# A graph-attention layer with residual and norm: x of the last four blocks loaded earlier, top-8 and largest norm moved in the drain, the stores of blocks 0 to 25 issued twice

## The chip, the core and the metric

One core of a Trainium2 chip. The metric is the time of one execution in microseconds (us), the median of several runs. A profiled run also gives the span, from the first to the last instruction; here a run's time is mostly 1.9 us above its span. The drain is what comes after the last turn of the loop over the blocks. All runs used here are in the fast state.

## The reference

```python
def reference(x, adj, L0_gnn_W, L0_gnn_a):      # x 4096 x 512, adj 4096 x 4096, all float32
    ht  = (x @ W).reshape(N, 4, 512)            # four heads
    e   = leaky_relu(src_i + dst_j) + adj       # adj up to 1e9: the largest entry of a row decides
    att = softmax(e, axis=-1)
    out = layernorm(x + (att @ ht).mean(heads))
```

Entries of adj reach 1e9. On this data the largest one of a row is so far ahead that softmax is 1 there and 0 elsewhere. The kernel therefore finds the column of each row's largest entry, gathers that row of x, multiplies it by the mean of the heads' weights, adds x and normalizes. A test at the end, which needs the two largest entries of each row and a bound from the norms of x, decides whether a slow general path must run. It does not run on this data.

## The kernel before

The 4096 rows are 32 blocks of 128. Per block: VectorE takes the maximum of each of 64 segments (`segment_maxima`), finds the leading segment, GpSimd gathers it, VectorE finds the column in it, GpSimd gathers that row of x as `y`, TensorE transposes `y` and multiplies it, ScalarE computes the statistics and writes the result over x in `hold`. Nearly all loads and stores are issued by SyncE, in program order. The code is cut and condensed:

```python
AHEAD, Q, PIECES, LATE = 5, 4, 4, NB - Q

def load_x(lo, n):
    nc.sync.dma_start(hold[:, ds(lo, n), :], x_rows[:, ds(lo, n), :])

def find_inner(ib):
    nc.vector.max(out=inner[:, ib, :], in_=lead_of[ib])          # top-8 of the leading segment

def find_column(ib):
    find_inner(ib)
    within = small.tile([P, 8], U32, name="within")
    nc.vector.max_index(within, inner[:, ib, :], lead_of.pop(ib))
    ...                                                          # column, then gather_rows

def store(queue, lo, n):
    queue.dma_start(out_rows[:, ds(lo, n), :], hold[:, ds(lo, n), :])
...
for t in range(NB):
    if t in x_at:
        load_x(*x_at[t])
    load_adj(t + AHEAD)
    ...

load_x(LATE, NB - LATE)                     # the drain begins here
for ib in range(NB - FINISH):               # blocks 0 to 25
    store(nc.sync, ib, 1)
find_column(NB - 2)
...
for ib in range(LATE, NB):
    row_norm(ib)                            # sums of squares of x, ScalarE
turn(NB - 2)
products(NB - 3, KB - 1, KB)
finish_last(NB - 4, True)                   # True: VectorE adds x first
find_inner(NB - 1)
bound(0)                                    # largest norm: VectorE reduces, TensorE transposes
products(NB - 2)
...
finish_last(NB - 2, True)
store(nc.sync, NB - 2, 1)
report(pg)
finish_last(NB - 1, False)
store(nc.scalar, NB - 1, 1)                 # the last store is issued by ScalarE
```

Of the kernel before, what the change touches and what calls it, by code (L numbers as in the profile page):

```python
# [65 lines left out]
def leading_rows(ctx, tc, x, adj, W, a, out, ident, v, n_bad, any_bad):  # L66
# [7 lines left out]
    nc = tc.nc  # L74
    N, D = x.shape
    H = a.shape[0]
    KB, NB, S = D // P, N // P, N // E
    AHEAD = 5
    Q = 4
    PIECES = 4  # L80
    LATE = NB - Q
# [20 lines left out]
    def pieces(ib):  # L102
        return PIECES if ib in (0, LATE, NB - 1) else 2 if ib > LATE else 1

    def load_adj(ib):
        if 0 <= ib < NB:
            t = adj_t[ib] = adj_pool.tile([P, N], F32, name="adj_t")
            n = pieces(ib)
            for k in range(n):
                nc.sync.dma_start(t[:, ts(k, N // n)], adj_rows[ib][:, ts(k, N // n)])  # L110

    def load_x(lo, n):
        nc.sync.dma_start(hold[:, ds(lo, n), :], x_rows[:, ds(lo, n), :])
# [26 lines left out]
    top = once.tile([P, NB, 8], F32, name="top")  # L140
    inner = once.tile([P, NB, 8], F32, name="inner")
# [5 lines left out]
    seg_of, at_of, lead_of, y_t, yt_of, o_ps = {}, {}, {}, {}, {}, {}  # L147

    def segment_maxima(ib, lo, hi):

        if lo == 0:
            seg_of[ib] = small.tile([P, S], F32, name="seg")
        n = max(pieces(ib), 2)
        for k in range(lo * n // PIECES, hi * n // PIECES):
            nc.vector.tensor_reduce(  # L155
                seg_of[ib][:, ts(k, S // n)],
                adj_t[ib][:, ts(k, N // n)].rearrange("p (s e) -> p s e", e=E), axis=AX.X, op=OP.max,
            )

    def find_segment(ib):  # L160
        seg = seg_of.pop(ib)
        nc.vector.max(out=top[:, ib, :], in_=seg)
        at = small.tile([P, 8], U32, name="at")
        nc.vector.max_index(at, top[:, ib, :], seg)  # L164
        row = small.tile([P, 1], U32, name="row")
        nc.gpsimd.tensor_tensor(row, at[:, 0:1], first[:, ib : ib + 1], op=OP.add)  # L166
        lead = small.tile([P, E], F32, name="lead")
        nc.gpsimd.indirect_dma_start(  # L168
            out=lead, out_offset=None, in_=adj_segs,
            in_offset=bass.IndirectOffsetOnAxis(ap=row[:, :1], axis=0),  # L170
        )
        start = at_of[ib] = small.tile([P, 1], U32, name="start")
        nc.gpsimd.tensor_tensor(start, at[:, 0:1], width, op=OP.mult)  # L173
        lead_of[ib] = lead

    def gather_rows(ib, col):
        y = y_t[ib] = rows.tile([P, D], F32, name="y", bufs=4)
        nc.gpsimd.indirect_dma_start(  # L178
            out=y, out_offset=None, in_=x,
            in_offset=bass.IndirectOffsetOnAxis(ap=col[:, :1], axis=0),  # L180
        )

    def find_inner(ib):
        nc.vector.max(out=inner[:, ib, :], in_=lead_of[ib])

    def find_column(ib):
        find_inner(ib)
        within = small.tile([P, 8], U32, name="within")
        nc.vector.max_index(within, inner[:, ib, :], lead_of.pop(ib))  # L189
        col = small.tile([P, 1], U32, name="col")  # L190
        nc.gpsimd.tensor_tensor(col, at_of.pop(ib), within[:, 0:1], op=OP.add)  # L191
        gather_rows(ib, col)

    def find_column_in_row(ib):

        col = small.tile([P, 8], U32, name="col")
        nc.vector.max_index(col, top[:, ib, :], adj_t[ib])
        gather_rows(ib, col)
# [9 lines left out]
    def residual(ib):  # L208
        o_ps[ib] = psum.tile([P, D], F32, name="o")
        nc.tensor.matmul(o_ps[ib], ident, hold[:, ib, :], start=True, stop=False)  # L210

    def products(ib, lo=0, hi=KB):
        start = ib not in o_ps
        if start:
            o_ps[ib] = psum.tile([P, D], F32, name="o")
        for kb in range(lo, hi):
            nc.tensor.matmul(  # L217
                o_ps[ib], yt_of[ib][:, kb, :], w_sum[:, kb, :],
                start=(start and kb == 0), stop=(kb == KB - 1),
            )  # L220

    def row_norm(ib):
        sq = rows.tile([P, D], F32, name="sq")
        nc.scalar.activation(sq, hold[:, ib, :], AF.Square, accum_out=xx[:, ib : ib + 1])  # L224
# [8 lines left out]
    def rstd(i):  # L233
        nc.gpsimd.tensor_scalar(sd[:, i], sd[:, i], 1.0 / D, EPS, op0=OP.mult, op1=OP.add)  # L234
        nc.gpsimd.tensor_tensor(sd[:, i], sd[:, i], power[:, : i.stop - i.start], op=OP.pow)  # L235
        nc.gpsimd.tensor_mul(nm[:, i], nm[:, i], sd[:, i])  # L236
# [5 lines left out]
    def finish_last(ib, residual):  # L242

        o = o_ps.pop(ib)
        if residual:
            nc.vector.tensor_add(hold[:, ib, :], o, hold[:, ib, :])
            o = hold[:, ib, :]
        st = small.tile([P, nc.vector.BN_STATS_DIM], F32, name="st", bufs=2)
        nc.vector.bn_stats(st, o)
        mv = small.tile([P, nc.vector.BN_AGGR_DIM], F32, name="mv", bufs=2)  # L250
        nc.vector.bn_aggr(mv, st)
        r = small.tile([P, 1], F32, name="r", bufs=2)
        nc.scalar.activation(r, mv[:, 1:2], AF.Sqrt, bias=eps)
        nc.vector.reciprocal(r, r)
        nc.vector.tensor_scalar(hold[:, ib, :], o, mv[:, 0:1], r, op0=OP.subtract, op1=OP.mult)  # L255

    def store(queue, lo, n):
        queue.dma_start(out_rows[:, ds(lo, n), :], hold[:, ds(lo, n), :])

    def mean_of_heads(kb):  # L260
        o = psum.tile([P, D], F32, name="o")
        for h in range(H):
            nc.tensor.matmul(o, ident, hold[:, w_at + kb * H + h, :], start=(h == 0), stop=(h == H - 1))  # L263
        nc.scalar.activation(w_sum[:, kb, :], o, AF.Copy, scale=1.0 / H)  # L264
# [43 lines left out]
    def bound(part):  # L308

        if part == 0:  # L310
            xm = once.tile([P, 1], F32, name="xm")
            nc.vector.tensor_reduce(xm, xx, axis=AX.X, op=OP.max)
            px = of_bound[0] = psum.tile([1, P], F32, name="px", bufs=1)
            nc.tensor.transpose(px, xm, ident)
        elif part == 1:
            nc.vector.tensor_reduce(xg, of_bound[0], axis=AX.X, op=OP.max)
            nc.scalar.activation(xg, xg, AF.Sqrt)
            pb = of_bound[1] = psum.tile([P, 1], F32, name="px", bufs=1)
            nc.tensor.matmul(pb, ones[0:1, :], xg, start=True, stop=True)
        else:  # L320
            nc.vector.tensor_mul(lead_by, of_bound[1], vn)
            nc.vector.tensor_scalar(lead_by, lead_by, 1.05, 110.0, op0=OP.mult, op1=OP.add)
# [28 lines left out]
    COLUMN, PROJECT, STATS, FINISH = 2, 3, 4, 6  # L351

    for t in range(NB):
        if t in x_at:
            load_x(*x_at[t])
        load_adj(t + AHEAD)
        middle = 1 if t == NB - 1 else 2
        segment_maxima(t, 0, middle)
        if t >= COLUMN:
            find_column(t - COLUMN)  # L360
        segment_maxima(t, middle, PIECES)
        find_segment(t)
        pair = t >= FINISH and t % 2 == 0
        if pair:
            rstd(slice(t - FINISH, t - FINISH + 2))
        if t < 2:
            mean_of_heads(t)
        elif t == 2:
            mean_of_heads(2)
            mean_of_heads(3)  # L370
        if t == 0:
            turn_a()
        turned = [(*vectors[0], turn_w(*vectors.pop(0))) for _ in range(vectors_at.get(t, 0))]
        if t == 16:
            head_norms()
        ib = t - PROJECT
        if ib >= 0:
            turn(ib)
            if ib < LATE:
                residual(ib)  # L380
        for some in turned:
            head_vector(*some)
        if ib >= 0:
            products(ib)
        if t >= STATS:
            stats(t - STATS)
            row_norm(t - STATS)
        if pair:
            finish(t - FINISH)
            finish(t - FINISH + 1)  # L390

    load_x(LATE, NB - LATE)
    for ib in range(NB - FINISH):
        store(nc.sync, ib, 1)
    find_column(NB - 2)
    rstd(slice(NB - FINISH, NB - FINISH + 2))
    find_column_in_row(NB - 1)
    turn(NB - 3)
    products(NB - 3, 0, KB - 1)
    finish(NB - FINISH)  # L400
    finish(NB - FINISH + 1)
    for ib in range(LATE, NB):
        row_norm(ib)
    turn(NB - 2)
    products(NB - 3, KB - 1, KB)
    finish_last(NB - 4, True)
    find_inner(NB - 1)
    bound(0)
    products(NB - 2)
    bound(1)  # L410
    finish_last(NB - 3, True)
    bound(2)
# [249 lines left out]
```

## Time and profile before

| | before |
|---|---|
| time, median | 247.81 us (first 3 runs), 247.84 (6 runs) |
| span of the profiled run | 245.3 us |
| moved by DMA | 97.77 MB, of it 8.39 written |
| DMA engines | full from the second to the 38th of 40 slices |
| TensorE / VectorE / ScalarE / GpSimd busy | 82 / 77 / 45 / 40% |

How to read it: the page cuts the span into 40 slices and gives the busy share in tenths, with the rate of the DMA engines below. "Windows" are the same for chosen stretches. "(x24)" counts 24 instructions, and the five engines of a windows line are TensorE, TensorE's weight loads, VectorE, ScalarE and GpSimd. SyncE only issues transfers, so its own time says little; what moves is seen in the rates. In a waits line stand the microseconds in total, the number of waits and the longest.

### The profile page before, as it was taken

Reading aid. Unit: us, or ns where it says so; the run is one execution under the profiler, and the core shown is the slowest. Engines: PE = TensorE matmul, PEld = TensorE weight load, DVE = VectorE, ACT = ScalarE, POOL = GpSimd, SP = SyncE. Lnnn points to the kernel's source line nnn. Section 1 sums busy time; section 2 is a strip of 40 time slices with the busy share of each in tenths; the row PEclk is TensorE's granted clock in tenths of the full one; section 3 lists DMA queues with packets and bytes.
Section 4 is the critical chain, followed back from the end, with each engine's and each line's share of the span. In section 5 each row is a group of like instructions: output and inputs, shape, how many; then the busy total and the mean of one; then the engine's idle time right before and its main releaser. Section 6 shows DMA issues by size and latency. Waiting matters only on the chain.

```text
span 245.3 us, 2538 instructions
## 1 busy us (share of the span) xinstructions
PE 200.4 (82%) x677; PEld 101.2 (41%) x678; DVE 188.7 (77%) x300; ACT 110.1 (45%) x266; POOL 97.6 (40%) x213
## 2 busy tenths in 40 slices
PE   0279948999999999999969777985969987987870
PEld 0135326555665555665334323332424432433320
DVE  2545686399689977998589979995998999966661
ACT  2012004044656565657645463744553846657110
POOL 1202423225616463646254535453455455652000
PEclk9999799599999999999999999999988999999995
DMA  7999999999999999999999999999999999999971
GB/s 257 435 428 414 422 423 425 418 424 408 425 416 415 415 414 422 422 402 431 418 418 413 426 412 421 408 424 416 416 414 390 412 408 400 409 401 376 402 294 55
DMA packets 16580, 97.77 MB, mean 399 GB/s; under 512 B 2472, under 2 KB 2472, under 8 KB 11184
## 3 DMA queue, kind: packets, MB, share of 16 engines
q1 hardware_dynamic: 12816, 87.82, 87.4%
q0 software_dynamic: 3584, 9.44, 10.0%
q10 hardware_dynamic: 160, 0.28, 0.3%
q8 instruction: 7, 0.11, 0.2%
q14 instruction: 13, 0.11, 0.1%
HBM read 89.15 MB, written 8.39 MB: 398 GB/s over the span
## 4 chain that ended last, share of the span: by engine, by line
DMA 35%; issue 26%; POOL 25%; DVE 7%; PE 4%; SPq 1%; POOLq 0%; ACT 0%; DVEq 0%
DMA adj_t<-in_adj_dram 29%; POOL y L178 8%; POOL lead L168 8%; DVE seg L155 5%; DMA lead<-in_adj_dram,row 3%; PE o L217 3%; DMA y<-in_x_dram,col 3%; POOL sd L235 3%; POOL row L166 2%; POOL start L173 2%; POOL col L191 1%; POOL sd L234 1%; POOL nm L236 1%; DVE hold L255 1%; SPq L110 1%
## 5 line engine op out<-in xcount | busy, mean ns | idle before, releaser
L155 DVE TENSOR_REDUCE seg<-adj_t 128x32 f32<-128x2048 f32 (+1 forms) x70 | 146.0, 2091 | 34.7 <-DMA adj_t<-in_adj_dram 34.5
L217 PE MATMUL o<-w_sum,yt 128*128 128x512 f32 x256 | 120.6, 613 | 1.3 <-ACT yt L206 1.3
L217 PEld LDWEIGHTS o<-w_sum,yt 128*128 128x128 f32 x256 | 47.1, 194 | 59.7 <-issue 47.0
L206 ACT COPY yt<-tp 128x512 f32<-128x512 f32 x32 | 18.8, 588 | 45.0 <-PE tp L204 44.9
L178 POOL DMA_INDIRECT y<-in_x_dram,col x32 | 32.2, 1008 | 16.7 <-POOL col L191 14.6
L168 POOL DMA_INDIRECT lead<-in_adj_dram,row x32 | 30.9, 964 | 15.5 <-POOL row L166 15.5
L204 PE MATMUL tp<-ident,y 128*128 128x128 f32 x128 | 19.7, 276 | 15.5 <-DMA y<-in_x_dram,col 15.3
L210 PE MATMUL o<-hold,ident 128*128 128x512 f32 x58 | 31.6, 627 | 0.8 <-DMA hold<-in_x_dram 0.8
L263 PE MATMUL o<-hold,ident 128*128 128x512 f32 x32 | 18.3, 724 | 15.7 <-DMA hold<-in_L_gnn_W_dram 15.7
L204 PEld LDWEIGHTS tp<-ident,y 128*128 128x128 f32 x128 | 14.4, 141 | 28.8 <-issue 27.4
L166 POOL TENSOR_TENSOR row<-at,first 128x1 uint32<-128x1 uint32 x32 | 5.9, 185 | 48.6 <-DVE at L164 47.4
L281 ACT COPY wt<-tp 128x512 f32<-128x512 f32 x16 | 9.2, 587 | 35.8 <-PE tp L279 35.8
L191 POOL TENSOR_TENSOR col<-start,within 128x1 uint32<-128x1 uint32 x31 | 5.9, 190 | 41.6 <-DVE within L189 41.6
L240 ACT ACTIVATE hold<-o,nm,sd 128x512 f32<-128x512 f32 x28 | 20.2, 771 | 2.5 <-POOL nm L236 2.5
L287 PEld LDWEIGHTS pv<-at_d,wt 128*128 128x128 f32 x128 | 17.2, 200 | 7.4 <-issue 3.9
L224 ACT ACTIVATE sq<-hold 128x512 f32<-128x512 f32 x32 | 19.8, 620 | 0.0
L231 ACT ACTIVATE sq<-o,nm 128x512 f32<-128x512 f32 x28 | 19.3, 688 | 0.9
L263 PEld LDWEIGHTS o<-hold,ident 128*128 128x128 f32 x32 | 7.2, 236 | 24.2 <-POOL row L166 10.4
L229 ACT ACTIVATE sq<-o 128x512 f32<-128x512 f32 x28 | 17.0, 607 | 0.0
L264 ACT ACTIVATE w_sum<-o 128x512 f32<-128x512 f32 x4 | 2.4, 598 | 31.7 <-PE o L263 31.7
L287 PE MATMUL pv<-at_d,wt 128*128 128x2 f32 x128 | 16.0, 249 | 0.6 <-ACT wt L281 0.6
L279 PEld LDWEIGHTS tp<-ident,hold 128*128 128x128 f32 x64 | 7.9, 142 | 6.9 <-issue 6.9
(73 smaller groups left out, 116.7 us busy)
## 6 DMA issues: line engine op xcount, KB each, us to landing
adj_t<-in_adj_dram SPq DMA_DIRECT2D x27, 2048.0 KB
out_dram<-hold SPq DMA_DIRECT2D x31, 256.0 KB
hold<-in_x_dram SPq DMA_DIRECT2D x7, 1024.0 KB
adj_t<-in_adj_dram SPq DMA_DIRECT2D x12, 512.0 KB
hold<-in_L_gnn_W_dram SPq DMA_DIRECT2D x4, 1024.0 KB
adj_t<-in_adj_dram SPq DMA_DIRECT2D x4, 1024.0 KB
hold<-in_x_dram SPq DMA_DIRECT2D x4, 256.0 KB
lead<-in_adj_dram,row POOLq DMA_INDIRECT x32, 5.8
```

The costliest lines, as they stand in the source:

```text
L155: nc.vector.tensor_reduce(seg_of[ib][:, ts(k, S // n)], adj_t[ib][:, ts(k, N // n)].rearrange("p (s e) -> p s e", e=E), axis=AX.X, op=OP.max,)
L168: nc.gpsimd.indirect_dma_start(out=lead, out_offset=None, in_=adj_segs, in_offset=bass.IndirectOffsetOnAxis(ap=row[:, :1], axis=0),)
L178: nc.gpsimd.indirect_dma_start(out=y, out_offset=None, in_=x, in_offset=bass.IndirectOffsetOnAxis(ap=col[:, :1], axis=0),)
L204: nc.tensor.transpose(tp[:, kb, :], y[:, ts(kb, P)], ident)
L206: nc.scalar.copy(yt, tp)
L210: nc.tensor.matmul(o_ps[ib], ident, hold[:, ib, :], start=True, stop=False)
L217: nc.tensor.matmul(o_ps[ib], yt_of[ib][:, kb, :], w_sum[:, kb, :], start=(start and kb == 0), stop=(kb == KB - 1),)
L224: nc.scalar.activation(sq, hold[:, ib, :], AF.Square, accum_out=xx[:, ib : ib + 1])
L231: nc.scalar.activation(sq, o, AF.Square, bias=nm[:, i], accum_out=sd[:, i])
L240: nc.scalar.activation(hold[:, ib, :], o_ps.pop(ib), AF.Identity, bias=nm[:, i], scale=sd[:, i])
L263: nc.tensor.matmul(o, ident, hold[:, w_at + kb * H + h, :], start=(h == 0), stop=(h == H - 1))
L287: nc.tensor.matmul(pv[:, kb, h : 2 * H : H], wt[:, k, :], at_d[:, k, h : 2 * H : H], start=(k == 0), stop=(k == KB - 1),)
```

## The change

The stated intent: x of the last four blocks comes in front of the last block of adj, so that TensorE can add it for block 28 within the loop; the top-8 of the late blocks' leading segments leaves the path of the searches; the reduction behind the largest norm runs before block 28's statistics, so that TensorE does not wait for it.

```diff
     def find_column(ib):
-        find_inner(ib)
+        if ib < LATE:
+            find_inner(ib)
         within = small.tile([P, 8], U32, name="within")
-        nc.vector.max_index(within, inner[:, ib, :], lead_of.pop(ib))
+        nc.vector.max_index(within, top[:, ib, :], lead_of[ib])
 ...
+        if t + AHEAD == NB - 1:
+            load_x(LATE, NB - LATE)
         load_adj(t + AHEAD)
 ...
-            if ib < LATE:
-                residual(ib)
+            residual(ib)
 ...
-    load_x(LATE, NB - LATE)
     for ib in range(NB - FINISH):
         store(nc.sync, ib, 1)
     find_column(NB - 2)
     rstd(slice(NB - FINISH, NB - FINISH + 2))
+    for ib in range(LATE, NB):
+        row_norm(ib)
+    for ib in range(NB - FINISH):
+        store(nc.sync, ib, 1)
     find_column_in_row(NB - 1)
 ...
-    for ib in range(LATE, NB):
-        row_norm(ib)
     turn(NB - 2)
     products(NB - 3, KB - 1, KB)
-    finish_last(NB - 4, True)
-    find_inner(NB - 1)
     bound(0)
     products(NB - 2)
+    finish_last(NB - 4, False)
+    for ib in range(LATE, NB):
+        find_inner(ib)
     bound(1)
```

## The prediction

> **What bounds the kernel now.** I read the page's strip of slices first, then its list of DMA issues, then the windows of the last stretch, and the chain of waits last. That order matters here: the chain alone points at the wrong resource for this change. The strip and the DMA parts of the page:
>
> ```profile
> DMA  7999999999999999999999999999999999999971
> GB/s 257 435 428 414 422 423 425 418 424 408 425 416 415 415 414 422 422 402 431 418 418 413 426 412 421 408 424 416 416 414 390 412 408 400 409 401 376 402 294 55
> DMA packets 16580, 97.77 MB, mean 399 GB/s; under 512 B 2472, under 2 KB 2472, under 8 KB 11184
> ...
> HBM read 89.15 MB, written 8.39 MB: 398 GB/s over the span
> ...
> out_dram<-hold SPq DMA_DIRECT2D x31, 256.0 KB
> ```
>
> The 16 DMA engines are full in every slice but the first and the last two (a slice is 245.3 / 40 = 6.13 us). TensorE (82% busy) and VectorE (77%) both have gaps. The output, 8.39 MB, is written once: 31 stores of 256 KB on SyncE's queue and one on ScalarE's. Every byte is moved at 400 to 425 GB/s from about 6 us to about 236 us, so until then time is bytes over bandwidth. How it ends is in the windows of the last stretch (columns: length, busy time of five engines, granted clock, DMA share, GB/s):
>
> ```profile
> 228.00:230.00 2.00, 1.53 (x5) 0.82 (x6) 1.60 (x6) 0.20 (x1) 0.00 (x0) 1.00 1.04 399
> 230.00:232.00 2.00, 2.00 (x6) 0.62 (x4) 1.27 (x4) 0.29 (x1) 0.00 (x0) 1.00 1.06 406
> 232.00:234.00 2.00, 2.00 (x10) 1.24 (x10) 1.38 (x9) 0.59 (x1) 0.00 (x0) 1.00 1.06 407
> 234.00:236.00 2.00, 2.00 (x6) 0.80 (x5) 1.53 (x5) 0.29 (x1) 0.00 (x0) 1.00 1.05 402
> 236.00:238.00 2.00, 1.79 (x6) 0.38 (x4) 1.07 (x5) 0.00 (x0) 0.00 (x0) 1.00 0.74 283
> 238.00:240.00 2.00, 0.00 (x0) 0.00 (x0) 1.57 (x4) 0.29 (x1) 0.00 (x0) 1.00 0.08 25
> 240.00:242.00 2.00, 0.00 (x0) 0.00 (x0) 0.11 (x1) 0.00 (x0) 0.00 (x0) 0.54 0.36 131
> ```
>
> These windows need care: from 228 to 236 us there is almost nothing on the DMA engines but stores, and they run at 399 to 407 GB/s with a share of 1.05, so the stores have a backlog that drains only at about 236.5 us. Only from there to 241 us does the end hang on computing. The chain of waits shows that part (start, length, what):
>
> ```profile
> 219.21 6.63 DMA y<-in_x_dram,col
> ...
> 227.65 0.55 DVE hold L255
> 228.19 0.14 DVE inner L184
> 228.33 0.10 DVE xm L312
> 228.42 0.04 issue
> 228.47 0.27 PE px L314
> 228.74 3.44 PE o L217 x8
> ...
> 239.30 0.81 DVE hold L255
> ```
>
> The reader should see two tails that end within some 4 us of each other: the backlog of stores (about 237 us) and the last block's chain of gather, transpose, products, statistics and store (data of the last store at 241 to 242 us). The chain names the second because it ends last; it does not say that the first is right behind it.
>
> **What the Trainium skill says.** "DMA: Bandwidth & Descriptors", section "Where 436 GB/s comes from", puts the ceiling of a core's DMA ports at 435 GB/s; the trace agrees (its best slice is 435, the long run from 6 to 190 us is 418, stores alone 403), so there is no spare rate to absorb added bytes. The same page, section "Issuing engines are not separate DMA queues", says that DMAs issued by several engines share the same 16 DMA engines; so the queue that issues added stores is no escape, which fits a share already at 1.0. "Perfetto Trace Analysis", the section on the HWDGE DMA instruction, says that the time of moving data is not within the issuing instruction's slice; here a store's slice on SyncE's queue is 0.58 us in the median, while the backlog shows only in the windows. The cost of added stores is therefore to be read in bytes, not in slices.
>
> **The change, part by part.**
>
> 1. *x of the last four blocks in front of the last block of adj.* The same 1 MB is read, in front of 2 MB of adj and not behind them. No byte is added. The last adj block can land up to 1.05 MB / 0.41 MB per us = 2.6 us later. In the trace the store that waits for the transfer of adj's last piece is issued at 213.5 us, and VectorE takes that piece at about 214.2 us: a margin near 0.7 us, so the last two gathers may go out up to 1.9 us later (estimate).
>
> 2. *x added by TensorE for block 28.* Two more matmul records (the pair costs 1.02 us in the timeline) inside the loop, where TensorE has gaps; it takes away one addition of 0.69 us on VectorE in the drain.
>
> 3. *The top-8 (MAX8) of the four late leading segments taken later.* Same instructions, 0.22 us each; three leave the path in front of the last column searches (-0.2 to -0.3 us each with its gap), and four now stand in the drain, where VectorE waits anyway. The column search now compares with the segment's maximum, same length.
>
> 4. *Largest norm without a wait.* The four squares of late rows (0.63 + 0.20 us each, 3.3 us) move ahead on ScalarE, to where it now sits idle 2.86 us before a copy, and the reduction that feeds the transpose runs before the block-28 statistics. TensorE's 1.01 us idle before that transpose (227.46 to 228.47) goes away: about -1.0 us on the last block's chain.
>
> Parts 1 to 4 move the computing tail by roughly -1.0 - 0.2 to that plus 1.9, so -1.2 to +0.7 us (estimate).
>
> 5. *What the short description doesn't say.* The diff adds, after the four moved squares, a second copy of the loop that stores blocks 0 to 25, while the first copy stays as context. The comparison of instruction orders confirms it: SyncE issues 57 stores in a row where it issued 31. The added 26 carry 26 x 262,144 B = 6.82 MB. They do not wait for computing (the blocks are long done), they are in front of the stores of blocks 26 to 30 on the same queue, and the DMA engines have no free time for them.
>
> Cost of part 5, from the windows: bytes moved in the kernel before from 236 us on are 2 x 283 + 2 x 25 + 2 x 131 and about 0.06 MB of later small traffic, together 0.94 MB. With the 6.82 MB there are 7.75 MB to move after 236 us. At the 403 GB/s of the store-only stretch that is 19.2 us: the data end at 255.2 us, against 241.8 us before (a finer window shows the last store's bytes between 241.0 and 242.0). From the last data to the end of the span the trace has about 3.5 us, which I keep. Span: 258.7 us, +13.4. The computing tail would be ready by 240 to 241 us, so its gain or loss is hidden under 14 us of stores. On the median: 247.81 + 13.4 = 261.2; I round to 261.0, because the stretch before 236 us may gain a little from a queue that never runs dry.
>
> **The rivals.**
>
> *The added stores are hidden, and the intended gain shows.* Then the span falls by about a microsecond, to 246.5 to 247 us. For it: stores are nowhere on the chain of waits. Against it: the DMA share is 1.0 in the very stretch where they would have to hide; free DMA time between 236 and 242 us is about 4 us, worth 1.6 MB, and I have counted it.
>
> *Full additive cost.* If the computing tail came after the backlog, 6.82 / 0.403 = 16.9 us would be added to all: 264.7 us. It would need the last gathers or the last store to be kept behind the backlog. The gathers go on another queue and in the kernel before they landed within 6.6 us under the same load; the last store is issued by ScalarE, not in SyncE's order. So only a small part of this is likely.
>
> *The issue of stores on SyncE becomes the bound.* 0.33 us is the shortest slice, 0.58 the median; 256 KB take 0.65 us at 403 GB/s. Issue keeps up, but each store also waits for the one eight before it (the instruction order shows eight semaphores in turn). Eight in flight are 2.1 MB or 5.2 us of transfers, enough to cover a landing. If it were slightly short of full rate, 380 GB/s would make it 262.3 us.
>
> *Stores alone run faster than 403*, say 425 as reads do: 254.2 us for the data, 260.2 us in all. The share of 1.05 in the store-only windows speaks against much of that.
>
> **Range and chances.** The size is a division of known bytes by a rate that the trace shows over 8 us of the same kind of traffic. The rate between 380 and 425 gives 260.2 to 262.3; the run-to-run spread (247.23 to 248.26) and a shift of the end by 1 us widen it: 258.5 to 263.7. Slower by over 2% means above 252.8 us, which fails only if over 60% of the added bytes cost nothing: 0.97. Within 2%: 0.02. Faster: 0.01.
>
> **What the changed profile would show.** Written bytes 15.2 MB in place of 8.39, total near 104.6 MB; 57 stores on SyncE's queue; DMA share near 1.0 at about 403 GB/s to about 254 us while TensorE and VectorE are idle from some 241 us; the chain ending in the stores' transfers, or in SyncE's wait for them. TensorE's 1.01 us wait before the norm's transpose gone. I am wrong if the rate after 240 us is far from 403, if the engines' last work moves beyond 245 us, or if the store-only stretch ends before 250 us.

## The result, and the profile after

265.69 us median (265.47 to 268.22, 6 runs) against 247.84 us (6 runs). The ratio is 1.0734, 95% interval 1.0686 to 1.0782. Here and below a ratio is the mean time of one kernel's fast runs over that of the other's of the same rounds, so not quite the ratio of the medians. The direction was as forecast, but the time is 2.0 us above the stated range and 4.7 above its centre.

The same lines of the page, for the changed kernel (a slice is 6.59 us):

```profile
DMA  7999999999999999999999999999999999994995
GB/s 258 436 423 431 404 416 434 415 413 420 414 418 414 418 425 415 418 414 426 418 415 423 415 416 408 425 413 420 386 411 408 402 402 406 396 399 154 358 382 198
DMA packets 20324, 104.58 MB, mean 397 GB/s; under 512 B 2888, under 2 KB 2888, under 8 KB 14928
...
HBM read 89.15 MB, written 15.20 MB: 396 GB/s over the span
...
out_dram<-hold SPq DMA_DIRECT2D x57, 256.0 KB
```

Bytes and counts are those of the prediction: 104.58 MB, 15.20 written, 57 stores on SyncE's queue. What was not foreseen is a hole: slice 37 has 154 GB/s. In windows (length, five engines' busy time, granted clock, DMA share, GB/s):

```profile
228.00:236.00 8.00, 8.00 (x24) 3.56 (x23) 6.43 (x23) 1.91 (x6) 0.00 (x0) 1.00 1.05 400
236.00:238.00 2.00, 1.81 (x6) 0.39 (x4) 1.28 (x6) 0.01 (x1) 0.00 (x0) 1.00 1.04 395
238.00:240.00 2.00, 0.00 (x0) 0.00 (x0) 1.57 (x4) 0.29 (x1) 0.00 (x0) 1.00 0.40 151
240.00:242.00 2.00, 0.00 (x0) 0.00 (x0) 0.14 (x1) 0.00 (x0) 0.00 (x0) 1.00 0.36 132
242.00:244.00 2.00, 0.00 (x0) 0.00 (x0) 0.00 (x0) 0.00 (x0) 0.00 (x0) 0.71 0.30 103
244.00:246.00 2.00, 0.00 (x0) 0.00 (x0) 0.00 (x0) 0.00 (x0) 0.00 (x0) 0.50 0.82 301
246.00:260.00 14.00, 0.00 (x0) 0.00 (x0) 0.00 (x0) 0.00 (x0) 0.00 (x0) 0.50 1.02 382
```

SyncE had 24 stores left to issue, yet from 238 to 246 us the DMA engines moved 2 x (151 + 132 + 103 + 301) = 1.37 MB, where 403 GB/s would have moved 3.22. The missing 1.85 MB are worth 4.6 us. And the rest runs at 382 and not at 403 GB/s.

Who held SyncE back is in the waits of its queue from 228 us on, and in its timeline, taken in two windows (from 236 to 242, and from 242 to 244):

```profile
SPq L260 <- DMA out_dram<-hold: 5.9, 1, 5.9
```

```profile
236.06 0.68 SPq L260 DMA_DIRECT2D out_dram<-hold  x1
```

```profile
242.68 1.43 SPq L260 DMA_DIRECT2D out_dram<-hold  x2
```

One single wait of 5.9 us: SyncE issues nothing from 236.74 to 242.68 us, and what ends the wait is the landing of a store. It is not one of its own, for the last packet of those ends at 240.16 us and their last count comes at 240.52. The only store landing then is the one of block 31, which ScalarE issues at 240.17 us and whose packets end at 242.06. The packed trace also has the semaphores: SyncE's store at 242.68 waits for number 107, which the built program calls DMAHW6 and block 31's store counts up, and its last count comes at 242.67 us.

The built program shows why SyncE waits for it. Each DMA that SyncE or ScalarE issues takes one of eight completion semaphores in turn, and first waits for the last DMA that used the same one. From the built instruction order (row, line, transfer, waits):

```
SyncE    80 L260 DMACopy out_dram<-hold 128x512 [waits DMAHW3, Activation]
         81 L260 DMACopy out_dram<-hold 128x512 [waits DMAHW4, Activation]
         82 L260 DMACopy out_dram<-hold 128x512 [waits DMAHW5, Activation]
         83 L260 DMACopy out_dram<-hold 128x512 [waits DMAHW7]
         ...
         89 L260 DMACopy out_dram<-hold 128x512 [waits DMAHW5]
         90 L260 DMACopy out_dram<-hold 128x512 [waits DMAHW6]
ScalarE 173 L260 DMACopy out_dram<-hold 128x512 [waits DMAHW6, DVE]
```

SyncE's turn skips DMAHW6 between rows 82 and 83: there the builder has put ScalarE's store of block 31, which in fact runs only at the very end. Seven stores later, at row 90, SyncE comes round to DMAHW6 and has to wait for block 31. No data asks for that. In the kernel before, ScalarE's store likewise took one turn (DMAHW4), but exactly seven SyncE stores followed it, so none came round to it.

The computing tail, from the chain of waits (start, length, what), stands where it was (239.33 against 239.30 us), so the time was not lost there:

```profile
221.01 5.96 DMA y<-in_x_dram,col
...
228.59 0.11 PE px L316
...
239.33 0.81 DVE hold L257
```

### The profile page after: what moved, and what is told of

It reads as the page before. It is cut to its first block, busy times and chain, and to the rows that moved or that the text cites. A ratio compares the mean times of both kernels' runs of the same rounds, so it can differ in the third digit from the quotient of the medians.

```text
span 263.7 us, 2547 instructions
## 1 busy us (share of the span) xinstructions
PE 197.7 (75%) x679; PEld 99.7 (38%) x680; DVE 185.7 (70%) x299; ACT 110.6 (42%) x266; POOL 97.3 (37%) x213
## 2 busy tenths in 40 slices
DMA packets 20324, 104.58 MB, mean 397 GB/s; under 512 B 2888, under 2 KB 2888, under 8 KB 14928
## 3 DMA queue, kind: packets, MB, share of 16 engines
HBM read 89.15 MB, written 15.20 MB: 396 GB/s over the span
## 4 chain that ended last, share of the span: by engine, by line
DMA 46%; POOL 17%; issue 16%; DVE 6%; PE 4%; SPq 0%; ACT 0%; POOLq 0%; DVEq 0%
DMA adj_t<-in_adj_dram 41%; DMA y<-in_x_dram,col 5%; DVE seg L155 5%; POOL lead L168 5%; POOL y L178 5%; PE o L219 3%; POOL sd L237 2%; POOL start L173 1%; POOL row L166 1%; POOL col L193 1%; PE tp L206 1%; POOL sd L236 1%; POOL nm L238 1%; SPq L110 0%; PE o L212 0%
## 5 line engine op out<-in xcount | busy, mean ns | idle before, releaser
L219 PE MATMUL o<-w_sum,yt 128*128 128x512 f32 x256 | 118.3, 604 | 0.7 <-ACT yt L208 0.7
L219 PEld LDWEIGHTS o<-w_sum,yt 128*128 128x128 f32 x256 | 46.3, 191 | 58.5 <-issue 45.7
L206 PE MATMUL tp<-ident,y 128*128 128x128 f32 x128 | 20.3, 282 | 17.7 <-DMA y<-in_x_dram,col 17.6
L289 PEld LDWEIGHTS pv<-at_d,wt 128*128 128x128 f32 x128 | 16.3, 191 | 6.8 <-ACT wt L283 3.5
L289 PE MATMUL pv<-at_d,wt 128*128 128x2 f32 x128 | 15.3, 244 | 0.6 <-ACT wt L283 0.6
L237 POOL TENSOR_TENSOR sd<-sd,power 128x2 f32<-128x2 f32 x14 | 10.1, 722 | 1.2
```

The costliest lines, as they stand in the source:

```text
L206: nc.tensor.transpose(tp[:, kb, :], y[:, ts(kb, P)], ident)
L219: nc.tensor.matmul(o_ps[ib], yt_of[ib][:, kb, :], w_sum[:, kb, :], start=(start and kb == 0), stop=(kb == KB - 1),)
L289: nc.tensor.matmul(pv[:, kb, h : 2 * H : H], wt[:, k, :], at_d[:, k, h : 2 * H : H], start=(k == 0), stop=(k == KB - 1),)
```

## The experiments

Theory A: a SyncE store waits for ScalarE's last store, because they share a completion semaphore. Theory B: the added bytes, or writing the same rows again, cost all of it. Twelve kernels ran in three jobs; "before" was run beside them each time (medians 247.46, 247.33 and 247.10 us).

| run | time us | ratio to before (95%) |
|---|---|---|
| e1_nodup | 246.79 | 0.9961 (0.9933 to 0.9989) |
| e2_dup_pool | 262.49 | 1.0595 (1.0556 to 1.0634) |
| e2_dup_sp | 262.28 | 1.0592 (1.0548 to 1.0635) |
| e3_before_dup1 | 249.66 | 1.0084 (1.0053 to 1.0114) |
| e4_after_dup1 | 246.67 | 0.9958 (0.9929 to 0.9987) |
| e5_norm_first | 248.96 | 1.0074 (1.0031 to 1.0117) |
| e5_norm_top8 | 247.69 | 1.0005 (0.9961 to 1.0050) |
| e6_dup_sp_warm | 266.61 | 1.0769 (1.0723 to 1.0815) |
| e7_norm_first_sp | 246.09 | 0.9959 (0.9937 to 0.9980) |
| e8_dup1_sp | 247.54 | 1.0013 (0.9993 to 1.0032) |
| e9_split_x_sp | 247.03 | 0.9977 (0.9948 to 1.0005) |
| e10_dup_other | 262.51 | 1.0613 (1.0588 to 1.0638) |

### e1_nodup: the change without the second store loop

```diff
-    for ib in range(NB - FINISH):
-        store(nc.sync, ib, 1)
     find_column_in_row(NB - 1)
```

> The changed kernel without the added second store loop. All theories hold that the loop alone makes the slowdown: 247.0 to 248.6 us against 247.84 before. The last block's chain should end within 0.3 us of before (in the changed kernel its last VectorE instruction started at 239.33 us against 239.30), so I expect no gain from the moved x, top-8 and norm together. If the moved parts matter by themselves, it is off by more than 1 us.

Measured: 246.79 us, ratio 0.9961. The second loop alone makes the slowdown. The stated parts of the change gain 0.4%, a little more than expected and below the 2% that would count.

### e2_dup_pool and e2_dup_sp: all the stores, no semaphore shared with ScalarE

```diff
-    store(nc.scalar, NB - 1, 1)
+    store(nc.gpsimd, NB - 1, 1)        # e2_dup_pool
+    store(nc.sync, NB - 1, 1)          # e2_dup_sp
```

> The changed kernel, all 57 stores kept, but the store of the last block is issued by GpSimd and no longer by ScalarE, so that it shares no completion semaphore with a store of SyncE's queue. Theory A (shared semaphore: a SyncE store waited 5.9 us for the last block's store): the gap in the stores from 238 to 244 us goes, span 257 to 258.5, time 259.0 to 260.5 us. Theory B (the gap or the loss comes from bytes alone, or from writing the same addresses again): no change, 265.2 to 266.2 us. The rate of the later stores, 381 GB/s in place of 403, should stay if it belongs to stores with idle engines, and rise if it came from the gap.

> The changed kernel, all 57 stores kept, and the store of the last block as the 58th on SyncE's queue in place of ScalarE's. The run with GpSimd issuing it had no gap, 262.5 us, with its own gather-queue traffic and a late end. Theory A (shared semaphore): no gap here either, 260.5 to 262.3 us. Theory B (gap from bytes or from writing the same rows again): 265.2 to 266.2 us. If the rate after 244 us is again near 382 GB/s, the lower rate has nothing to do with the gap.

Measured: 262.49 and 262.28 us. The windows of e2_dup_sp from 236 us on have no hole (same columns as above):

```profile
236.00:244.00 8.00, 1.54 (x5) 0.38 (x4) 2.80 (x8) 0.29 (x1) 0.00 (x0) 0.71 1.05 394
246.00:256.00 10.00, 0.00 (x0) 0.00 (x0) 0.00 (x0) 0.00 (x0) 0.00 (x0) 0.50 1.01 378
```

Theory A holds: same bytes, the hole is gone, and the ratio falls from 1.0734 to 1.0592, which is 0.0142 x 247.6 = 3.5 us. It is less than the 5.9 us wait, since in its first part the engines still moved the 0.79 MB left of the stores already issued (2.0 us at 403 GB/s), and less than the 4.6 us of the missing bytes, since the data of e2_dup_sp come late too: from 246 to 248 us it ran at 343 GB/s, and its last 0.11 MB took until 257.8 us (57 GB/s from 256 to 258). Why it ends so unevenly is open. The expectation for e2_dup_pool was missed by 2 us: its stores ran at 369 GB/s from 246 to 256 us and ended at 258.0 us. Most of the slowdown, 5.9 of 7.3%, stays without the hole: that is the cost of moving the added bytes.

### e3_before_dup1, e8_dup1_sp and e4_after_dup1: one added store

If theory A is right, 256 KB can cost more than 2 us or nothing, depending only on where the semaphores fall.

```diff
     for ib in range(NB - FINISH):
         store(nc.sync, ib, 1)
+    for ib in range(1):
+        store(nc.sync, ib, 1)           # e3: in the kernel before; e8: the same
 ...
-    store(nc.scalar, NB - 1, 1)
+    store(nc.sync, NB - 1, 1)           # e8 only
```

e4_after_dup1 is the changed kernel with its second loop cut to `range(1)`.

> The kernel before with one single added store (block 0 again, 256 KB). In the built order the last SyncE store, of block 30, then falls on the semaphore of ScalarE's store of block 31. Theory A (shared semaphore): that store is issued only at about 242.7 us and the time rises to about 250.4 us (+2.6). Theory B (bytes only): 0.26 MB are worth 0.65 us at most, 247.8 to 248.5 us.

> The changed kernel with the added loop cut to one single store (block 0 again). In the built order six SyncE stores follow the semaphore of ScalarE's store, so none waits for it. Theory A (shared semaphore) and theory B (bytes only) both expect 247.5 to 248.7 us, within 0.7 us of the same kernel without any added store; if theory A's pairing is wrong and any added store costs over 2 us, it shows here.

> The kernel before with one added store of block 0 (249.66 us when ScalarE issued block 31's store), now with block 31's store on SyncE's queue. Same bytes, same number of stores. Theory A: 247.0 to 248.0 us, the 2.2 us are gone. Theory B (the added bytes cost 2.2 us): still 249.3 us or more.

Measured: 249.66 (e3), 246.67 (e4) and 247.54 us (e8). The timeline of e3 after 238 us ends with these two issues; block 30's store, whose rows were ready at 236.28 us, goes out after block 31's:

```profile
239.94 0.39 ACTq L258 DMA_DIRECT2D out_dram<-hold  x1
242.55 0.33 SPq L258 DMA_DIRECT2D out_dram<-hold  x1
```

The waits of SyncE's queue from 228 us on, first in e3, then in e8:

```profile
SPq L258 <- DMA out_dram<-hold: 7.8, 3, 7.1
```

```profile
SPq L258 <- DMA out_dram<-hold: 1.2, 4, 0.4
```

The same added 256 KB cost 0.84% where the turn of semaphores comes round to ScalarE's store (e3), and nothing that can be told from noise where it does not (e8: 0.13%, interval 0.9993 to 1.0032; e4 against e1: 0.9958 and 0.9961). This is theory A's doing and not the bytes'. (e4 lies 0.8 us below its stated band, which left out the 0.4% that e1 gained.) The built programs show the turns: in e3 eight SyncE stores follow ScalarE's turn and the eighth takes its semaphore, in e4 six follow.

### e5_norm_first, e7_norm_first_sp and e5_norm_top8: the norm's wait by itself

```diff
+    bound(0)
+    products(NB - 2)
     finish_last(NB - 4, True)
     find_inner(NB - 1)
-    bound(0)
-    products(NB - 2)
 ...
-    store(nc.scalar, NB - 1, 1)
+    store(nc.sync, NB - 1, 1)           # e7 only
```

e5_norm_top8 has the first move and the late top-8 of the change, on the kernel before.

> The kernel before with one move alone: the reduction and transpose of the largest norm ahead of block 28's statistics. TensorE's 1.0 us wait before that transpose should go and the last block's chain end about 1 us sooner, at 239.1 us. But in the built order the last SyncE store (block 30) now falls on the semaphore of ScalarE's store of block 31, as in the run with one added store, which cost 2.2 us. Theory A (shared semaphore): 247.46 - 1.0 + 2.2, so 248.2 to 249.2 us, with SyncE's last store issued after 241 us. Rival (the wait gone is all that counts): 246.2 to 246.8 us.

> The kernel before with the norm's reduction moved first (as in the earlier run that measured 248.96 us) and the last block's store on SyncE's queue, so that block 30's store shares no semaphore with a later one of another queue. Theory A (the shared semaphore ate the gain of the removed wait): SyncE's store of block 30 is issued near 236 us and not at 241.8, the last block's chain ends near 238.4 us as it did there, and the time is 246.0 to 246.9 us. Rival (the moved reduction itself is slower): 248.5 us or more.

> The kernel before with the norm moved as in the run above and the late top-8 taken in the drain, without the moved x and without TensorE's addition for block 28. In the built order no store follows on the shared semaphore. Theory A: the 1.0 us wait is gone at no price and the three top-8 are off the path of the searches, 245.9 to 246.8 us against 247.46, that is at least as good as the changed kernel without the added stores (246.79), because the last adj block is not delayed. Rival: the gain of that run came from the moved x and TensorE's addition, then 247.2 to 247.8 us here.

Measured: 248.96 us (e5_norm_first), 246.09 (e7) and 247.69 (e5_norm_top8). In e5_norm_first the move did its work: the last block's chain ended 0.9 us sooner (its last VectorE instruction started at 238.40 us against 239.30). Yet the kernel is slower, because the move also shifted the builder's turn of semaphores by one, and block 30's store came to wait for block 31's. Its timeline ends:

```profile
238.40 0.81 DVE L255 TENSOR_SCALAR hold<-o,mv,r 128x512 f32<-128x512 f32 x1
239.24 0.39 ACTq L258 DMA_DIRECT2D out_dram<-hold  x1
241.83 0.33 SPq L258 DMA_DIRECT2D out_dram<-hold  x1
```

With the last store on SyncE (e7) the gain comes through: 246.09 us, ratio 0.9959. It is a version faster than both kernels, but it cannot be told from e1 and e4. (The last store on SyncE without any other move was not run; e8, which has it with one added store, gained nothing.) e5_norm_top8 missed its expectation. Its chain in the profiled run goes through VectorE from 230 to 240 us, with four top-8 instructions beside the addition that it keeps for block 28, and its last VectorE instruction starts at 239.92 us. But this execution also had a granted TensorE clock of 0.50 from 218 to 220 us, where e5_norm_first had 1.00, and its transposes of block 29 came at 223.07 us against 221.39. Its runs spread from 246.38 to 249.01 us. Whether the late top-8 pays without TensorE's addition for block 28 is therefore not shown.

### e9_split_x_sp: less x in front of the last adj block

```diff
-            load_x(LATE, NB - LATE)
+            load_x(LATE, 1)
 ...
+    load_x(LATE + 1, NB - LATE - 1)
     for ib in range(NB - FINISH):
```

Also without the second loop, and with the last store on SyncE.

> The changed kernel without the added stores, with x of block 28 alone in front of the last adj block (256 KB), x of blocks 29 to 31 behind it, and the last store on SyncE's queue. Meant as the version that keeps all the intended gains: the last gathers, which landed 1.0 us later with 1 MB in front (226.9 against 226.0 us), should land as before, and the norm's wait stays gone. I expect the last block's chain to end about 238.2 to 238.7 us and 245.7 to 246.5 us, better than 246.79. If the delay of the gathers does not come from the moved x, it is the same 246.8.

Measured: 247.03 us, ratio 0.9977, no gain over e1. In its profiled run the gather of block 30 was issued at 219.58 us (221.01 in e1, 219.21 before), so the delay by the moved x is gone. Still the last VectorE instruction starts at 239.06 us (238.99 in e1). The chain names ScalarE, which squares the late rows of x until the copy of block 29's transposes starts at 223.57 us (221.77 in e1); but these transposes end only at 223.40 us (in e1 they begin at 221.10), so the squares delay the copy by 0.2 us at most. TensorE was late: its eight products from 213.10 us took 5.04 us at a granted clock of 0.50 to 0.65, where such a group takes 3.68 at 1.00. So this trace doesn't tell what the split is worth; it stays open.

### e6_dup_sp_warm and e10_dup_other: why the late stores are slower

```diff
     store(nc.sync, NB - 1, 1)
+    warm = psum.tile([P, D], F32, name="px", bufs=1)      # e6
+    for _ in range(24):
+        nc.tensor.matmul(warm, ident, w_sum[:, 0, :], start=True, stop=True)
 ...
     for ib in range(NB - FINISH):
-        store(nc.sync, ib, 1)                             # e10: second loop, to another tensor
+        nc.sync.dma_start(other[:, ds(ib, 1), :], hold[:, ds(ib, 1), :])
```

> The same as the run with 58 stores on SyncE's queue, and 24 matmuls without use after the last block, so that TensorE works until about 257 us. Theory C (the stores slow from 403 to 382 GB/s because the engines are idle and the granted clock is 0.5): the rate stays at 395 to 405 GB/s after 244 us and the time falls by 0.6 to 1.0 us against that run. Theory D (the lower rate belongs to something else): same rate, about 382, and the same time within 0.3 us.

> The changed kernel with its 26 added stores sent to another, unused tensor in memory, and the last store on SyncE's queue: the same bytes and count as the run with 58 stores on SyncE's queue (262.28 us). It asks for the cause of the lower rate of the late stores (378 to 391 GB/s after 244 us against 402 before). Theory E (writing the same rows a second time is slower): 398 to 405 GB/s and 261.3 to 261.8 us. Theory F (late stores alone are slower whatever they write): 378 to 391 GB/s and 262.0 to 262.6 us.

Measured, the window from 246 to 256 us of e6 and of e10:

```profile
246.00:256.00 10.00, 10.00 (x25) 4.43 (x24) 0.00 (x0) 0.00 (x0) 0.00 (x0) 1.00 1.02 383
```

```profile
246.00:256.00 10.00, 0.00 (x0) 0.00 (x0) 0.00 (x0) 0.00 (x0) 0.00 (x0) 0.50 1.03 385
```

TensorE was kept at clock 1.00 in e6, and the stores went at 383 GB/s; with other rows as target in e10, at 385 (378 in e2_dup_sp, with the dip of 343). Neither the idle TensorE and its clock (theory C) nor the second writing of the same rows (theory E) makes the lower rate. Why stores run at about 400 GB/s until some 240 to 244 us and mostly at 377 to 392 after it stays open. e10 also has a dip of its own, 300 GB/s from 240 to 244 us: one SyncE store issued at 239.29 us took 2.15 us, with no wait for another store listed. Its cause is open too. The time of e6, 266.61 us, does not bear on this: its stores end like those of e2_dup_sp, but its last added matmul ends at 258.05 us and its span 4.8 us after that, and its measured times are 3.6 to 3.9 us above the span, which I have no cause for.

## Why the prediction was wrong

- **DMA as the bound, bytes of the second loop, chance of slower: right.** 104.58 MB, 15.20 written, 57 stores; e1_nodup shows that the loop alone makes the slowdown.
- **Parts 1 to 4 neutral within -1.2 to +0.7 us and hidden: right.** The chain ended at the same place. Part 1 delayed the gather of block 30 from 219.21 to 221.01 us, +1.8 against "up to 1.9", and part 4 took the wait of TensorE away. Without the added stores the sum is -0.4% (e1). One reading is loose: not every byte moves at 400 to 425 GB/s up to 236 us, for there are slices of 376, 390 and 431 to 435, and 380 from 220 to 228 us; the sum doesn't use it.
- **The step that failed** is in the dismissal of the rival "full additive cost": "the last store is issued by ScalarE, not in SyncE's order. So only a small part of this is likely." I had seen the eight semaphores in turn, and took them as a limit within SyncE's queue. I did not ask who else takes a turn. The rival feared that the last store is kept behind the backlog; it was the backlog that was kept behind the last store. "Eight in flight", 5.2 us of transfers, was no cover either: 0.79 MB, 2.0 us, were left when SyncE stopped. A store of SyncE waited 5.9 us for ScalarE's store, the DMA engines starved for the worth of 4.6 us, and the computing tail and the remaining stores came one after the other in place of overlapping. The kernels without the shared semaphore, 262.28 and 262.49 us, are within the predicted range.
- **A term mis-sized:** the rate. From 246 us on it was 382 and not 403 GB/s; 14 us at 382 move 5.35 MB, which takes 13.3 us at 403: +0.7 us. The prediction named 380 GB/s only for a SyncE that issues too slowly; here the engines were busy all the while (DMA share 1.02). The cause of the rate is open.
- **The sum:** predicted span 258.7, + 4.6 for the hole, + 0.7 for the rate up to 260 us, is 264.0 (an estimate); the trace has 263.7. The small rest is in the end after the last data: from the last store's last packet it is 2.7 us here and 3.2 in the kernel before.

## What to carry to other kernels

When transfers are issued from two queues, list which completion semaphore each takes and ask who comes round to it: a late store on one queue can hold up ready stores on another, and a move elsewhere in the kernel can shift that pairing. A long chain of waits that ends in computing does not show a store backlog that drains just before it; read the rates of the last stretch. And read the whole diff for work done twice before pricing what its description names.

## What the Trainium skill lacked or had wrong

- "DMA: Bandwidth & Descriptors", section "Issuing engines are not separate DMA queues": it says that issuing from several engines only saves time on the sequencer. It lacks that queues whose transfers share completion semaphores (here the builder gave them out in turn) can block each other: SyncE's stores stood still for 5.9 us behind ScalarE's last store, which cost 3.5 us, and one added store of 256 KB cost 0.84% or nothing depending on the pairing.
- The same page, section "Why a DMA increments its semaphore by 16 and not by 1", advises "One semaphore per in-flight slot, not one per stream." as a matter of right data. That the slot's next user then waits for the former one, on whichever queue that is, is not said (7.1 us in e3_before_dup1).
- The same page, section "Where 436 GB/s comes from": the sentence that for transfers between HBM and SBUF the HBM side (~358 GB/s) binds is too general as it stands. This core ran at 418 GB/s from 6 to 190 us, near the 425 GB/s that the same section gives for the page's own 16 MB measurement, taken with the pair's other core idle. No run here shows what the other core of the pair did.
- No page has the rate of stores alone: 400 to 403 GB/s from 228 to 236 us, and mostly 377 to 392 after about 244 us, whether TensorE works or not and whichever rows are written.
